# Layer 1's projection for pairs of tiles: seven block products in place of eight

## The chip, the cores and the metric

The kernel runs on one core of one Trainium2 chip. A core has TensorE (PE; its weight loads are shown apart as PEld), VectorE (DVE), ScalarE (ACT), GpSimd (POOL), SyncE (SP) that issues ordinary transfers, and 16 DMA engines which all queues share. SBUF is the working memory, PSUM is where TensorE writes[...]. The metric is the device time of one execution in microseconds; before the change the median of three runs is 1902.05 (1896.26 to 1904.1). The profile is of one further execution that took 1954.92.

## The reference

Two graph-attention layers with a residual and a layer norm each, over N = 3327 nodes with D = 1024 features. `adj` is a 0/1 matrix of some 16 neighbours a node, with a full diagonal.

```python
# layer 0: 8 heads of 128
h = (x @ W).reshape(C, H, D)
e = alpha_src[:, :, None] + alpha_dst[:, None, :]      # then leaky relu, -inf where adj == 0
out = jnp.einsum('hij,hjd->hid', softmax(e), h_heads)
x = _layernorm(x + out)
# layer 1: one head of 1024
h = input @ W
f1 = h @ a1; f2 = h @ a2
attention = softmax(where(adj > 0, leaky_relu(f1 + f2.T), neg), axis=1)
x = _layernorm(x + relu(attention @ h))
```

Since attention @ (x @ W) = (attention @ x) @ W, the kernel aggregates layer 1's inputs first and projects the result.

## The kernel before, in words

Rows are worked on in NT = 26 tiles of P = 128. The program has three stages: a projection for layer 0 that also turns `adj` into lists of neighbours (to about 480 us of the profile), layer 0 (to about 1223), and layer 1 (to the end). A fourth, dense branch isn't taken on this input. All order is written by hand (`tc.manual_schedule()`): each engine gets its instructions in the order in which the program emits them and works on them in that order, waiting on semaphores.

Layers 0 and 1 have one frame, `pipeline` (L1058 on). A tile's neighbours come in four blocks of 4 x 128 rows and one last block of 128 (b = 0 to EB = 4). In the loop of tile t, step b does this, in this order: at b = 0 it closes tile t-1; at b = 2 it prepares tile t+1; it makes the weights of the next block (`weights(b + 1)`, on VectorE, or block 0 of tile t+1 at b = 4); it sums the block (`sums(b)`, on TensorE); it fetches block b of tile t+1 (`fetch`, indirect gathers on POOL, L817, into five buffers); and it runs pieces of the work that is left from tile t-1, written as generators: `run(work, behind[b])` advances it by so many steps. A second queue, `ahead`, is advanced by one step after each block.

In layer 1 (`class Target`, L960):

- `prepare` (L966): a transpose on TensorE of the tile's scores (L969), Exp on ScalarE into `way`, a PSUM bank (L971), the 0/1 marks of the targets on VectorE (`marks`, L833 and L837), and the load of the tile's own row of `y_d` into `res` (L976, SP). `own` has another Exp (L982).
- `weights` (L994): three VectorE operations, two in `way` (L1001, L1002) and one into `es` (L1004).
- `sums` (L1007): 12 matmuls (24 records) for blocks 0 to 3, three (six records) for block 4, into three banks `acc` of tag "A", which has five; the thirds come in the order 2, 0, 1 (L1013).
- `close` (L1018): three small VectorE operations (L1021 to L1023), three ScalarE scalings of `res` into `z` (L1027), three VectorE operations that add the sums (L1030). A third of `acc` is free once its L1030 has read it.
- `finish` (L1035): `z` is transposed in two halves (L176 on TensorE, L179 on ScalarE, one bank of tag "T"), and projected with `wt1`, the 1024 x 1024 weights: for each half of the columns eight matmuls of 128x128 by 128x512 into the one bank of tag "S" (L1045), in pieces of two; then relu and residual in one VectorE operation (L1048) into `o`, a buffer of tag "z".
- `settle` (L1053), queued in `ahead`: the layer norm by `norm_steps` (statistics L192 to L194 and a Sqrt on ScalarE L195 in the first step; reciprocal and normalization, L197 and L199, in the second), then the output DMA on SP.

The call `pipeline(Target, 1, (2, 2, 2, 2, 1), ...)` gives ten pieces a loop: the two transposes after block 0, four matmuls after each of the blocks 1 to 3, two after block 4, and two more after the next tile's `close`.

`score_weights` (L781), queued in `ahead` at the beginning of layer 0, multiplies `wt1` by layer 1's two score vectors, and puts them into `wa`, which layer 0's `finish` uses (L951). Layer 0's tiles use two banks of tag "A" each and one of "S".

Of the kernel before, what the change touches and what calls it, by code (L numbers as in the profile page):

```python
# [9 lines left out]
F32 = mybir.dt.float32  # L10
# [3 lines left out]
AF = mybir.ActivationFunctionType  # L14
OP = mybir.AluOpType
# [4 lines left out]
P = 128  # L20
# [6 lines left out]
def kernel(  # L27
# [28 lines left out]
    nc = tc.nc  # L56
# [100 lines left out]
    class Phase:  # L157
# [10 lines left out]
        def sbuf(self, tag, shape, bufs, name=None, dt=F32):  # L168
            return self.pool.tile(shape, dt, tag=tag, name=name or tag, bufs=bufs)
# [571 lines left out]


    def sparse(own):
        ph = Phase(own, "sparse", {"A": 5, "S": 1, "T": 1, "E": 1})
        pool, bank, sbuf = ph.pool, ph.bank, ph.sbuf
        NS = 5
        srcs = [pool.tile([P, NG, HG], F32, bufs=1, name=f"src{n}") for n in range(NS)]
# [28 lines left out]


        wc = pool.tile([P, 2, KT], F32, bufs=1, name="wc")
        wa = [pool.tile([P, D], F32, bufs=1, name=f"wa{n}") for n in range(2)]

        def score_weights():  # L781
            for n, a in enumerate((a1_src, a1_dst)):
                av = sbuf("z", [P, D], 3, "av")
                spread(av, a)
                for k in range(KT):
                    pr = sbuf("pr", [P, D], 1)
                    nc.vector.scalar_tensor_tensor(
                        pr, wt1[:, k, :], 1.0, av, op0=OP.mult, op1=OP.mult, accum_out=wc[:, n, k : k + 1]
                    )
                    if k % 3 == 2:  # L790
                        yield
                for g in range(2):
                    tr = bank("T", [P, 4, P], "tr")
                    for k in range(4):
                        nc.tensor.transpose(
                            tr[:, k, :], wc[:, n, 4 * g + k : 4 * g + k + 1].to_broadcast([P, P]), ident
                        )
                    nc.scalar.activation(wa[n][:, g * HALF : (g + 1) * HALF], tr.rearrange("p a b -> p (a b)"), AF.Copy)
                yield
# [40 lines left out]
        class Layer0:  # L840
# [5 lines left out]
            def prepare(self):  # L846
                self.re = listed.pop(self.t)
                self.oh, self.oh2 = marks(self.t)
                self.y = ys[self.t % 3]
                load_rows(self.y[:, :D], x, self.t)  # L850
                self.h = sbuf("own", [P, HW0], 2)
                nc.sync.dma_start(self.h, h0_d[self.t * P : (self.t + 1) * P, :])

            def own(self):
# [17 lines left out]
            def weights(self, b):  # L872

                s = self.src[b]
                ng, wide = (NG, GT) if b < EB else (1, P)
                blk = slice(b * NG, b * NG + ng)
                oh = self.oh[:, blk, :] if b < EB else self.oh2.unsqueeze(1)
                wp = way[:, (b % 4) * NG * H : (b % 4 * NG + ng) * H].rearrange("p (g h) -> p g h", g=ng)
                nc.vector.tensor_tensor(wp, s[:, :, D : D + H], self.re[:, blk, :], OP.mult)
                nc.vector.tensor_tensor(wp, wp, s[:, :, D + H : D + 2 * H], OP.max)  # L880
                w = sbuf("w", [P, NG, H], 4)
                nc.scalar.activation(w, wp if b < EB else wp.to_broadcast([P, NG, H]), AF.Copy)  # L882
                e = sbuf("e", [P, H * P], 3).rearrange("p (g h t) -> p g h t", g=ng, h=H)
                nc.vector.tensor_tensor(  # L884
                    e, oh.unsqueeze(2).to_broadcast([P, ng, H, wide]),
                    wp.unsqueeze(3).to_broadcast([P, ng, H, wide]), OP.mult,
                )
                self.made[b] = w, e
# [42 lines left out]
            def finish(self):  # L931

                met = sbuf("met", [NG * H, P], 2)
                nc.vector.tensor_tensor(met, self.den[: NG * H, :P], meets, OP.mult)
                nc.tensor.matmul(self.den[:, P:], met, heads, start=True, stop=True)  # L935
                yield
                ri = sbuf("ri", [P, H], 2)
                nc.vector.tensor_tensor(ri, self.den[:, P:], self.es, OP.add)  # L938
                nc.vector.reciprocal(ri, ri)
                t, row = self.t, self.y  # L940
                y = row[:, :D]
                for h in range(H):
                    yh = y[:, h * DH : (h + 1) * DH]
                    nc.vector.scalar_tensor_tensor(
                        yh, self.acc[h // 4][:, h % 4, :], ri[:, h : h + 1], yh, op0=OP.mult, op1=OP.add
                    )
                yield
                yield from ph.norm_steps([y])
                for n in range(2):
                    pr = sbuf("pr", [P, D], 1)  # L950
                    nc.vector.scalar_tensor_tensor(  # L951
                        pr, y, 1.0, wa[n], op0=OP.mult, op1=OP.mult, accum_out=r1.sd[:, t, n, :]
                    )
                    if n == 0:
                        yield
                nc.scalar.activation(row[:, D + 1 : D + 2], r1.d[:, t, :], AF.Exp)
                nc.scalar.activation(row[:, D + 2 : D + 3], r1.d[:, t, :], AF.Exp, scale=SLOPE)
                nc.sync.dma_start(y_d[t * P : (t + 1) * P, :], row)

        class Target:  # L960
# [4 lines left out]

            def prepare(self):  # L966
                t = self.t
                tr = bank("T", [P, P], "tr")
                nc.tensor.transpose(tr, r1.s[:, t, :].to_broadcast([P, P]), ident)  # L969
                self.r = way[:, (t % 2) * P : (t % 2 + 1) * P].rearrange("p (g t) -> p g t", g=NG)  # L970
                nc.scalar.activation(  # L971
                    self.r.rearrange("p g t -> p (g t)"), tr, AF.Exp, scale=1 - SLOPE
                )
                self.oh, self.oh2 = marks(t)
                self.res = ys[t % 3]
                nc.sync.dma_start(self.res, y_d[t * P : (t + 1) * P, :])  # L976

            def own(self):
# [10 lines left out]
                self.src[b] = gather(y_d, HW, self.t, b)  # L989

            def begin(self):
                self.acc = [bank("A", [P, CUTS[1]], "acc1") for _ in range(3)]

            def weights(self, b):  # L994
                s = self.src[b]
# [22 lines left out]
            def close(self):  # L1018
# [2 lines left out]
                nc.vector.tensor_tensor(ri[:, 2:3], self.acc[2][:, D - CUTS[2] : D - CUTS[2] + 1], self.es[:, :1], OP.add)  # L1021
                nc.vector.reciprocal(ri[:, :1], ri[:, 2:3])
                nc.vector.tensor_tensor(ri[:, 1:2], ri[:, :1], self.es[:, :1], OP.mult)  # L1023
                z = self.z = sbuf("z", [P, D], 3)
                for c in (2, 0, 1):
                    cut = slice(CUTS[c], min(CUTS[c + 1], D))
                    nc.scalar.activation(z[:, cut], self.res[:, cut], AF.Copy, scale=ri[:, 1:2])  # L1027
# [6 lines left out]

            def finish(self):  # L1035

                t, z, res = self.t, self.z, self.res
                xT = sbuf("xT", [P, KT, P], 2)
                yield from ph.transposed(xT, z, (0, 1))
                o = sbuf("z", [P, D], 3, "o")  # L1040
                for g in range(2):
                    half = slice(g * HALF, (g + 1) * HALF)
                    acc = bank("S", [P, HALF], "mm")
                    for k in range(KT):
                        nc.tensor.matmul(acc, xT[:, k, :], wt1[:, k, half], start=k == 0, stop=k == KT - 1)  # L1045
                        if k in (1, 3, 5):
                            yield
                    nc.vector.scalar_tensor_tensor(o[:, half], acc, 0.0, res[:, half], op0=OP.max, op1=OP.add)  # L1048
                    if g == 1:
                        ahead.append(self.settle(o))  # L1050
                    yield

            def settle(self, o):  # L1053
                yield from ph.norm_steps([o])
                for r in pieces(self.t):
                    nc.sync.dma_start(out[at(self.t, r), :], o[r])

        def pipeline(kind, late, behind, get):  # L1058

            tiles = [kind(t) for t in range(NT)]
            work = deque()
            get(0)
            tiles[0].prepare()
            for b in range(EB + 1):
# [2 lines left out]
            for t, tg in enumerate(tiles):  # L1070
                tg.begin()
                for b in range(EB + 1):
                    if b == 0 and t:
                        tiles[t - 1].close()
                        run(work, late)
                    if b == 0 and t + 1 < NT:
                        get(t + 1)
                    if b == 2 and t + 1 < NT:
# [7 lines left out]
                    tg.sums(b)  # L1086
                    if t + 1 < NT:
                        tiles[t + 1].fetch(b)
                    run(work, behind[b])
                    if t or b:  # L1090
                        run(ahead)
                if t == 0 and late:
                    work.append(iter(range(1)))
                work.append(tg.finish())
            tiles[-1].close()
            run(work, late)
            run(ahead, -1)
            run(work, -1)
            run(ahead, -1)

        with tc.manual_schedule():
            pipeline(Layer0, 0, (1, 1, 1, 1, 1), get_edges)
            pipeline(Target, 1, (2, 2, 2, 2, 1), lambda t: None)


    def by_pairs(own):
# [145 lines left out]
```

## Time and profile before

| what | value |
|---|---|
| median of three runs | 1902.05 us |
| the profiled execution | 1954.92 us, its span 1953.2 us |
| busy, whole span | PE 1668.2 us (85%), DVE 1151.9 (59%), ACT 546.6 (28%), POOL 1039.7 (53%) |
| granted TensorE clock, mean | 0.907 |
| projection matmuls of layer 1 (L1045) | 832 records, 382.3 us busy, 603 ns each, overlapping |
| sums of layer 1 (L1013), blocks 0 to 3 | 2496 records, 215.9 us busy |
| gathers of layer 1 (L817) | 416 and 26, 1002 and 990 ns of POOL each |
| data read from and written to HBM | 578.85 and 42.97 MB |

A record is one hardware instruction; an fp32 matmul has two. Times of matmuls overlap each other, so what a group of them costs is read from its start to the next group's. The chain of waits is followed back from the last instruction: each entry was released by the one before it, so an engine that fills the chain sets the time. "Idle before" in a group's row counts only where nothing else was late. "Granted clock" is the share of the full TensorE clock in a stretch.

### The profile page before, as it was taken

To read this page: it belongs to the slowest core of one execution; us is meant where nothing else is said; L and a number is where in the kernel's file an instruction comes from. 1 tells how busy PE (TensorE), PEld (TensorE's weight loads), DVE (VectorE), ACT (ScalarE), POOL (GpSimd) and SP (SyncE) were. 2 spreads that over 40 slices of the span, in tenths; PEclk is the share of its full clock that TensorE was granted. 3 is DMA by queue.
4 is the path that set the end of the run, shared out by engine and by line. 5 is a ranking of instruction groups with operands and counts; after the bars stand their busy time and mean duration, and the time that the engine had idled before them with its cause. 6 is when DMAs were issued, how large, how long until landed. Compare 5 with 4: busy or idle time off the path is not lost.

```text
span 1953.2 us, 36865 instructions
## 1 busy us (share of the span) xinstructions
PE 1668.2 (85%) x14091; PEld 915.1 (47%) x14091; DVE 1151.9 (59%) x3087; ACT 546.6 (28%) x1422; POOL 1039.7 (53%) x1391
## 2 busy tenths in 40 slices
PE   8799999997577787777877777479999999999997
PEld 5456555564444554544454445134444444444343
DVE  6699989985575566556665566134444444444442
ACT  5445554442122222222222222012122222222221
POOL 4322222211666666666666663566666666666650
PEclk9899999998677887879787887589999999999999
DMA  7556554311999999999999996899999999999980
GB/s 183 95 129 130 112 94 92 88 60 64 404 356 377 370 365 387 381 372 363 379 377 375 369 371 225 335 318 386 378 378 367 381 366 373 357 377 368 355 340 32
DMA packets 171063, 567.68 MB, mean 291 GB/s; under 512 B 27690, under 2 KB 34346, under 8 KB 170878
## 3 DMA queue, kind: packets, MB, share of 16 engines
q0 software_dynamic: 131056, 455.68, 67.3%
q1 hardware_dynamic: 39822, 109.56, 15.1%
q8 instruction: 113, 1.85, 0.4%
q14 instruction: 72, 0.59, 0.1%
HBM read 578.85 MB, written 42.97 MB: 318 GB/s over the span
## 4 chain that ended last, share of the span: by engine, by line
PE 74%; issue 10%; DVE 6%; ACT 5%; DMA 2%; another core or an unknown queue 1%; POOL 1%; SPq 0%; POOLq 0%; DVEq 0%; ACTq 0%
PE mm L1045 19%; PE acc L914 19%; PE acc L1013 13%; PE mm L479 12%; PE acc L906 4%; PE acc L896 3%; ACT junk L311 3%; PE tr L176 2%; DMA wt<-in_L_gnn_W_dram 1%; DMA src<-h_d,idx 1%; PE den L922 1%; PE xp L411 1%; DVE top L274 1%; PE den L935 1%
## 5 line engine op out<-in xcount | busy, mean ns | idle before, releaser
L817 POOL DMA_INDIRECT src<-h_d,idx x416 | 448.9, 1079 | 228.0 <-PE acc L914 83.1
L817 POOL DMA_INDIRECT src<-y_d,idx x416 | 416.8, 1002 | 250.9 <-issue 84.4
L914 PE MATMUL acc<-src,e 128*32 128x128 f32 x6656 | 396.2, 321 | 167.0 <-issue 138.1
L914 PEld LDWEIGHTS acc<-src,e 128*32 128x32 f32 x6656 | 254.1, 127 | 332.5 <-issue 309.4
L479 PE MATMUL mm<-wt,xT 128*128 128x347 f32 (+1 forms) x1248 | 402.0, 468 | 3.0 <-DMA wt<-in_L_gnn_W_dram 2.6
L1045 PE MATMUL mm<-wt,xT 128*128 128x512 f32 x832 | 382.3, 603 | 3.1 <-DVE o L1048 3.1
L479 PEld LDWEIGHTS mm<-wt,xT 128*128 128x128 f32 x1248 | 228.2, 192 | 105.5 <-issue 4.0
L1013 PE MATMUL acc<-src,es 128*32 128x342 f32 (+1 forms) x2496 | 215.9, 467 | 39.2 <-DVE es L1004 24.9
L1045 PEld LDWEIGHTS mm<-wt,xT 128*128 128x128 f32 x832 | 151.9, 190 | 201.6 <-issue 184.9
L884 DVE TENSOR_TENSOR e<-oh,way 128x1024 f32<-128x1024 f32 x130 | 158.7, 1221 | 110.0 <-ACT w L882 29.5
L1013 PEld LDWEIGHTS acc<-src,es 128*32 128x32 f32 x2496 | 73.6, 112 | 171.5 <-issue 163.4
L882 ACT ACTIVATE w<-way 128x32 f32<-128x32 f32 x130 | 25.0, 193 | 449.1 <-PE acc L914 177.2
L1027 ACT ACTIVATE z<-y,ri 128x342 f32<-128x342 f32 (+1 forms) x78 | 39.5, 569 | 290.5 <-issue 118.7
L1001 DVE TENSOR_TENSOR way<-way,src 128x128 f32<-128x128 f32 x104 | 31.1, 299 | 147.2 <-ACT way L971 57.1
L1048 DVE SCALAR_TENSOR_TENSOR o<-mm,y 128x512 f32<-128x512 f32 x52 | 35.9, 691 | 108.9 <-PE mm L1045 73.9
L179 ACT ACTIVATE xT<-tr 128x512 f32<-128x512 f32 x104 | 59.4, 596 | 128.0 <-PE tr L176 115.0
L906 PE MATMUL acc<-own,ident 128*128 128x512 f32 x104 | 81.0, 871 | 0.0
L311 ACT ACTIVATE junk<-ad 128x3328 uint8<-128x3328 uint8 x26 | 78.4, 3014 | 2.5 <-POOL ad L308 2.5
L1021 DVE TENSOR_TENSOR ri<-acc,es 128x1 f32<-128x1 f32 x26 | 4.1, 158 | 124.3 <-PE acc L1013 116.7
L938 DVE TENSOR_TENSOR ri<-den,es 128x8 f32<-128x8 f32 x26 | 4.3, 166 | 119.8 <-PE den L935 119.8
L296 POOL CAST mvs<-r 128x8 bf16<-128x8 f32 x26 | 6.1, 235 | 122.8 <-ACT r L295 122.8
L864 ACT ACTIVATE own<-own,es 128x128 f32<-128x128 f32 x208 | 63.6, 388 | 26.2 <-DVE es L861 16.0
(194 smaller groups left out, 2020.8 us busy)
## 6 DMA issues: line engine op xcount, KB each, us to landing
h_d<-ht SPq DMA_DIRECT2D x26, 520.0 KB
own<-h_d SPq DMA_DIRECT2D x26, 520.0 KB
y_d<-y SPq DMA_DIRECT2D x26, 514.0 KB
y<-y_d SPq DMA_DIRECT2D x26, 514.0 KB
x<-in_x_dram SPq DMA_DIRECT2D x25, 512.0 KB
y<-in_x_dram SPq DMA_DIRECT2D x25, 512.0 KB
out_dram<-o SPq DMA_DIRECT2D x25, 512.0 KB
ad<-in_adj_dram POOLq DMA_DIRECT2D x25, 415.9 KB
```

The lines of the kernel that those rows point to most:

```text
L179: nc.scalar.activation(part, tr, AF.Copy)
L311: nc.scalar.activation(junk, ad, AF.Copy, accum_out=self.deg)
L479: nc.tensor.matmul(acc, xT[t][:, k, :], wt[:, k, CUTS0[c] : CUTS0[c + 1]], start=k == 0, stop=k == KT - 1)
L817: nc.gpsimd.indirect_dma_start(out=s[:, g, :w], out_offset=None, in_=table[:, :], in_offset=bass.IndirectOffsetOnAxis(ap=idx[:, t, b * NG ...
L864: nc.scalar.activation(hn, hn, AF.Copy, scale=es[:, n : n + 1])
L884: nc.vector.tensor_tensor(e, oh.unsqueeze(2).to_broadcast([P, ng, H, wide]), wp.unsqueeze(3).to_broadcast([P, ng, H, wide]), OP.mult,)
L896: nc.tensor.matmul(self.acc[h // 4][:, h % 4, :], e[:, 0, h, :], rowsof[:, 0, h, :], start=False, stop=h % 4 == 3,)
L906: nc.tensor.matmul(self.acc[b - 1].rearrange("p h d -> p (h d)"), ident, self.h[:, (b - 1) * HALF : b * HALF], start=False, stop=False,)
L914: nc.tensor.matmul(self.acc[h // 4][g * GT : (g + 1) * GT, h % 4, :], e[:, g, h, :], rowsof[:, g, h, :], start=first and h % 4 == 0, stop= ...
L1013: nc.tensor.matmul(self.acc[c][to, :m], es[:, g, :], s[:, g, CUTS[c] : CUTS[c + 1]], start=b == 0, stop=b == EB,)
L1027: nc.scalar.activation(z[:, cut], self.res[:, cut], AF.Copy, scale=ri[:, 1:2])
L1045: nc.tensor.matmul(acc, xT[:, k, :], wt1[:, k, half], start=k == 0, stop=k == KT - 1)
```

## The change

For two tiles a (even) and b (odd), the rows of a and b, cut into two halves of the 1024 inputs, are a 2 x 2 matrix of blocks, and so are the weights (w11, w12, w21, w22, each 512 x 512). The plain product needs eight products of blocks, each four matmuls; the change uses a Strassen form with seven (28 matmuls for a pair instead of 32), with sums and differences of blocks before and after them:

- `combine_weights`, once between the layers on VectorE: t3 = w22 - w12, w12 becomes w12 - w11, t2 = w22 - w12 (new), t4 = w21 - t2; w12 is overwritten in place. The other results lie in buffers that layer 0 has done with (`e`, `prod`, `own`), which therefore become named tiles.
- The even tile does two products, a1 w11 and a2 w21, and can put its first half at once. The odd tile does five, with s1 = b1 + b2, s2 = s1 - a1, b1 = a1 - b1, and s2 = a2 - s2 as new left operands, and puts its own halves and the even tile's second.
- `put` replaces L1048 by two VectorE operations: the sum of two partial results (one in PSUM) and the relu with the residual, in place in `res`. So `o` goes; `z` has one buffer; the residual rows have five (the three `ys` and the two `wa` of layer 0).
- Tag "A" has four banks in place of five, "S" two in place of one. `acc` takes its banks in the order 2, 0, 1. The transpose of `prepare` writes a part of `way`.
- `pipeline` takes a plan: for even and odd t, and for six places (after `close`, and after each block), which left-over tile is advanced: "even" and "odd" are the last tile of each kind that is complete. An even tile's six pieces run over loops t+1 and t+2, an odd tile's twelve over t+1 and t+2. After the last tile, two more rounds of the plan are run.

```diff
-        ph = Phase(own, "sparse", {"A": 5, "S": 1, "T": 1, "E": 1})
+        ph = Phase(own, "sparse", {"A": 4, "S": 2, "T": 1, "E": 1})
...
+        def combine_weights():
+            for n in range(2):
+                k = slice(2 * n, 2 * n + 2)
+                nc.vector.tensor_tensor(t3[n], w22[:, k, :], w12[:, k, :], OP.subtract)
+            nc.vector.tensor_tensor(w12, w12, w11, OP.subtract)
+            for n in range(2):
+                k = slice(2 * n, 2 * n + 2)
+                nc.vector.tensor_tensor(t2[n], w22[:, k, :], w12[:, k, :], OP.subtract)
+                nc.vector.tensor_tensor(t4[n], w21[:, k, :], t2[n], OP.subtract)
...
             def prepare(self):
                 t = self.t
-                tr = bank("T", [P, P], "tr")
+                tr = way[:, 3 * P :]
...
-                self.res = ys[t % 3]
+                self.res = y1s[t % len(y1s)]
...
-                self.acc = [bank("A", [P, CUTS[1]], "acc1") for _ in range(3)]
+                self.acc = {c: bank("A", [P, CUTS[1]], "acc1") for c in (2, 0, 1)}
...
             def finish(self):
...
-                acc = bank("S", [P, HALF], "mm")
-                for k in range(KT):
-                        nc.tensor.matmul(acc, xT[:, k, :], wt1[:, k, half], start=k == 0, stop=k == KT - 1)
-                    nc.vector.scalar_tensor_tensor(o[:, half], acc, 0.0, res[:, half], op0=OP.max, op1=OP.add)
...
+                self.xT = sbuf("xT", [P, KT, P], 2)
+                turn = ph.transposed(self.xT, self.z, (0, 1))
+                next(turn)
+                yield
+                next(turn)
+                yield from self.second() if self.t % 2 else self.first()
+
+            def product(self, a, w):
+                self.p = bank("S", [P, HALF], "mm")
+                for k in range(HK):
+                    nc.tensor.matmul(self.p, a[:, k, :], w(k), start=k == 0, stop=k == HK - 1)
+                    if k == 1:
+                        yield
+
+            def put(self, g, u, p, room):
+                half = slice(g * HALF, (g + 1) * HALF)
+                nc.vector.tensor_tensor(room, u, p, OP.add)
+                nc.vector.scalar_tensor_tensor(
+                    self.res[:, half], room, 0.0, self.res[:, half], op0=OP.max, op1=OP.add
+                )
+
+            def first(self):
+                yield
+                yield from self.product(self.xT, lambda k: w11[:, k, :])
+                nc.scalar.activation(u2, self.p, AF.Copy)
+                yield
+                yield from self.product(self.xT[:, HK:, :], lambda k: w21[:, k, :])
+                self.put(0, u2, self.p, u4)
+                yield
+
+            def second(self):
+                before = tiles1[self.t - 1]
+                a, b = before.xT, self.xT
+                a1, a2, b1, b2 = a[:, :HK, :], a[:, HK:, :], b[:, :HK, :], b[:, HK:, :]
+                nc.vector.tensor_tensor(s1, b1, b2, OP.add)
+                nc.vector.tensor_tensor(s2, s1, a1, OP.subtract)
+                nc.vector.tensor_tensor(b1, a1, b1, OP.subtract)
+                yield
+                yield from self.product(s2, lambda k: t2[k // 2][:, k % 2, :])
+                nc.vector.tensor_tensor(u2, u2, self.p, OP.add)
+                nc.vector.tensor_tensor(s2, a2, s2, OP.subtract)
+                yield
+                yield from self.product(s1, lambda k: w12[:, k, :])
+                p5 = self.p
+                nc.vector.tensor_tensor(u4, u2, p5, OP.add)
+                yield
+                yield from self.product(b1, lambda k: t3[k // 2][:, k % 2, :])
+                nc.vector.tensor_tensor(u3, u2, self.p, OP.add)
+                self.put(1, u3, p5, u2)
+                yield
+                yield from self.product(b2, lambda k: t4[k // 2][:, k % 2, :])
+                self.put(0, u3, self.p, u3)
+                ahead.append(self.settle())
+                yield
+                yield from self.product(s2, lambda k: w22[:, k, :])
+                before.put(1, u4, self.p, u4)
+                ahead.append(before.settle())
+                yield
...
-        def pipeline(kind, late, behind, get):
+        def pipeline(tiles, plan, get):
+            left = []
+
+            def rest(t, n):
+                for who in plan[t % 2][n]:
+                    k = {"before": t - 1, "even": t - 2 + t % 2, "odd": t - 1 - t % 2}[who]
+                    if 0 <= k < len(left):
+                        next(left[k], None)
...
                         tiles[t - 1].close()
-                        run(work, late)
+                        rest(t, 0)
...
-                    run(work, behind[b])
+                    rest(t, b + 1)
...
+            for t in (NT, NT + 1):
+                for n in range(EB + 2):
+                    rest(t, n)
+                    run(ahead)
             run(ahead, -1)
...
-            pipeline(Layer0, 0, (1, 1, 1, 1, 1), get_edges)
-            pipeline(Target, 1, (2, 2, 2, 2, 1), lambda t: None)
+            one = ("before",)
+            pipeline([Layer0(t) for t in range(NT)], (((),) + (one,) * 5,) * 2, get_edges)
+            combine_weights()
+            tiles1 = [Target(t) for t in range(NT)]
+            y1s = ys + was
+            e, o = "even", "odd"
+            pipeline(
+                tiles1, (((e,), (o, e), (o, e), (o, o), (o, o), ()), ((o, o), (e, o), (e, o), (o,), (o, e), ())),
+                lambda t: None,
+            )
```

## The prediction

> **What bounds the kernel now.** I began with the page's busy tenths. Layer 1 is the last third of the span.
>
> ```profile
> PE   8799999997577787777877777479999999999997
> PEclk9899999998677887879787887589999999999999
> DMA  7556554311999999999999996899999999999980
> ```
>
> In layer 1 TensorE and the DMA engines are both at nine tenths, at full clock, so two resources compete to be the bound. The chain of waits over one tile tells which one it is (start us, length, what):
>
> ```profile
> 1587.68 3.43 PE mm L1045 x8
> 1591.11 1.86 PE acc L1013 x24
> 1592.97 0.59 PE tr L176 x4
> 1593.56 0.69 issue
> 1594.25 0.66 PE tr L176 x4
> ...
> 1600.40 0.11 PE tr L969
> ...
> 1611.49 1.73 PE acc L1013 x6
> 1613.22 0.86 PE mm L1045 x2
> ```
>
> The chain never leaves TensorE: a tile is 25.54 us (1587.68 to 1613.22), with one stall of 0.69 us between the two transposes. An fp32 matmul shows as two records, so 3.43 us is four matmuls: 0.857 us each. A group of four that directly follows the sums takes 3.63. How near DMA is, and how the clock reacts to idleness, come from stretches of the trace (length; busy us of PE, PEld, DVE, ACT, POOL; granted clock, DMA share, GB/s):
>
> ```profile
> 1331.19:1586.63 255.44, 247.81 (x1428) 106.04 (x1427) 114.02 (x330) 58.37 (x100) 170.07 (x170) 1.00 0.99 374
> ...
> 1248.90:1252.30 3.40, 1.44 (x10) 0.49 (x7) 1.69 (x5) 0.00 (x0) 2.48 (x4) 1.00 1.02 406
> 1252.30:1255.70 3.40, 1.81 (x3) 0.28 (x3) 0.00 (x0) 0.00 (x0) 2.79 (x3) 0.50 1.02 406
> ...
> 1839.30:1842.70 3.40, 1.79 (x4) 0.87 (x5) 2.36 (x7) 0.00 (x0) 1.94 (x2) 1.00 1.04 420
> ```
>
> Ten tiles move 374 x 255.44 = 95.5 MB, 9.55 MB a tile. At the 408 GB/s that backlogged stretches reach, the DMA floor is 23.4 us a tile: TensorE is the bound by only 2.1 us. PE busy for 1.44 of 3.40 us was followed by a stretch at half clock; the stretch with 1.79 of 3.40 still had the full clock, and so had what followed.
>
> **What decides on VectorE.** The third view is the timeline around one tile's preparation:
>
> ```profile
> 1622.69 1.28 ACT L971 ACT_TABLE_LOAD   x1
> ...
> 1629.50 0.26 ACT L971 ACTIVATE way<-tr 128x128 f32<-128x128 f32 x1 [5.53 <-PE acc L1013]
> 1629.80 0.30 DVE L1001 TENSOR_TENSOR way<-way,src 128x128 f32<-128x128 f32 x1 [5.36 <-issue]
> ```
>
> In nearly every tile the weights of block 3 (L1001 to L1004, 0.95 us) start 0.03 us after ScalarE's Exp for the next tile (L971), which itself needs a table load after a Sqrt. Today nothing is lost: sums(3) stands behind four matmuls. The page's row for the operation that the change multiplies:
>
> ```profile
> L1048 DVE SCALAR_TENSOR_TENSOR o<-mm,y 128x512 f32<-128x512 f32 x52 | 35.9, 691 | 108.9 <-PE mm L1045 73.9
> ```
>
> [...] 691 here, 1221 for the 1024-wide L884. [...]
>
> **The change, part by part**, for a pair of tiles (before: 2 x 25.54 = 51.08 us).
>
> TensorE: 28 matmuls for 32: -4 x 0.857 = -3.43. The two transposes of a tile come in different blocks, so the 0.69 us stall goes: -1.38. Groups directly behind sums fall from six to four (-0.4), and six two-matmul groups appear, which may cost as much: 0.
>
> VectorE: 15 operations of 512 replace 4: 10.4 us for 2.8, +7.6 a pair. Busy goes from 45% to some 60%: not a bound, but it is in order, and three places matter.
>
> 1. Odd loop, after product 4 (in block 1). VectorE: start 0.1, add 0.72, relu-add 0.72, then at once the settling's statistics (1.7), done at 3.24. ScalarE: Sqrt to 3.5, Exp table 1.28, Exp 0.26, to 5.1. Then weights(3) 0.95: sums(3) can start at 6.15. TensorE meanwhile has L969 0.11, sums(2) 1.86, and just one half product, 1.91: 3.88. Stall 2.27. Were the Exp not waited for, VectorE's own order (statistics, marks 1.0, weights) still gives 5.2: stall 1.3.
> 2. Odd to even. After product 5: put 1.54, statistics 1.7, weights(0) 0.95, reciprocal and norm 1.0: `close` starts at 5.2 and frees its first bank at 6.95 (three small operations 0.58, z 0.61 and 0.57 later). TensorE arrives at the second third of sums(0), which with four banks needs that bank, at 1.75 + 1.73 + 1.71 + 0.62 = 5.81. Stall 1.2.
> 3. Even loop, block 0: u2's copy (0.6) and a table load precede the Exp of `own`, so weights(1) is late by 0.3.
>
> Other blocks have slack: in the even loop sums(3) could start at 6.8 and is reached at 8.1; product 4's bank is free at 5.1 for 6.0. Stalls are 3.77, so a pair takes 51.08 - 4.81 + 3.77 = 50.04: -1.04, over 12 pairs **-12.5**.
>
> Clock: a gap of 2.27 us takes over 1.8 us out of one window (below the 0.52 busy that was tolerated) in (1.14 + 0.94)/3.41 = 61% of positions: 7 of 12 gaps. A half-speed window loses 1.7: **+11.9** (0 if such gaps are tolerated, +41 if each of the 12 costs two windows).
>
> Start: loop 1 had groups of 4.28, 3.63 and 3.63 (chain, from 1288.56); one half group of 1.9 and a moved transpose (about 1) stay. Its gathers were all issued by 1275.5, so the gain is real: **-8.5** (0 if DMA still holds the loop). The work isn't saved, it moves to the end.
>
> End: before, from the last tile's sums (1922.78) to the end of the last normalization (1948.70) 25.9. After, in order: half product 1.86, wait for the late z 2.6, transposes 1.24, two half products 3.42, wait for s2 0.4, three products 10.3, wait for the bank that p5 holds 1.6, two products 6.86, then VectorE: remains of one settling 1.1, put 1.54, statistics 1.7, Sqrt 0.3, norm 1.0. Together 33.9: **+8.0** (+6 to +11).
>
> At nothing: combining the weights (6 x 1.22 + 2.29 = 9.6 us of VectorE) falls where VectorE waits 15.17 us for the first gather (1238.88); uncovered, +9.6. Layer 0 with four banks uses two a tile, freed two blocks into the next; two S banks and its new plan issue the same steps: 0, at most 1 us a tile. SP issues the same DMAs; both outputs of a pair now leave within one odd loop, behind that loop's load of y: 1 MB, 2.6 us of DMA, covered by the four blocks of gathers in flight. POOL is 17 x 1.29 = 21.9 us a tile, unchanged.
>
> Sum: -12.5 + 11.9 - 8.5 + 8.0 = -1.1 on the profiled 1954.92 (span 1953.2), which stands 2.8% above the median 1902.05. Scaled: **1901**.
>
> **Rivals.** (B) *The stalls are covered.* For it: VectorE is 45% busy and I priced each operation at its full length, while the trace shows starts 0.61 apart. Against: the chain at 1 is fixed by dependencies. A pair would take 46.27, 23.1 a tile; DMA's 23.4 takes over, realistically 23.5: -2.04 x 24 = -49, 1854; with half the stalls 1878.
> (C) *Slower, by the clock.* Every gap at place 1 pulls the clock down for two windows: 12 x 3.4 = +41, less 12.5: 1929. For it: layer 0, with PE 77% busy, was granted 0.81. Against: TensorE is busy right after each gap. Each window costs 1.7 us, so the loops' gain is gone at 7 windows, and from 13, more than one a pair, it is slower.
> (D) *DMA sets the pace* and the removed matmuls change nothing: loops 0, start 0, end +8, 1910. For it: the share of 0.99. Against: the chain holds no gather, and POOL waits for PE to free buffers.
>
> **Chances.** A measurement of this kernel tells about 0.5%, 9.5 us: faster below 1892.5, slower above 1911.5. A, the forecast, 0.45 (own range 1888 to 1914: 0.09 faster, 0.27 same, 0.09 slower). B 0.24, faster. C 0.26 (0.24 slower). D 0.05 (0.04 same). Faster 0.33, same 0.33, slower 0.34. Range 1864 to 1926: it leaves out the lower half of B and the top of C.
>
> **What would show it.** Right: in odd loops L1013 waits about 2 us for L1004 once a pair; in even loops about 1 us for the z operations of `close` (L1030); the clock at 0.5 now and then in layer 1; a pair near 51 us with the drops; DMA share below 0.99. Wrong: a steady clock of 1.00 and a pair at 47 (B), DMA named as the releaser ahead of L1004 (D), or waits of TensorE for a product's bank in every loop, which I price at 0.

## The result, and the profile after

The kernel after the change takes 1897.69 us (median of 12 runs, 1892.61 to 1902.04), the kernel before 1900.43 (12 runs, 1896.26 to 1904.1): a ratio of 0.9988 [0.9977, 0.9999]. The forecast was 1901. The 2.7 us between them are less than the 0.5% below which the prediction calls two times the same.

Chips differ here, and it matters for what follows. The first group of experiments below comes from a chip on which the kernel before takes 1948 us; all other runs, those of after included, come from chips on which it takes 1900. For the profile of before that the prediction worked from (1954.92 us) no chip is on record; its layer 0 takes 746.9 us, near the 740.6 of that first chip and not the 712 to 723 of all others, so it most likely comes from there. The kernel before was not profiled on a chip where it takes 1900, so what is said of its loops and its end is measured on the slower one. Every experiment's ratio compares runs on one chip.

The profiled execution of after took 1897.84 us, its span 1896.1. Its page, in busy tenths of 40 slices (the last 15 slices are layer 1):

```profile
PE   8799999999356666766766656389999999999997
PEclk9899999999688878878787888599999999999999
DMA  7666455411899999999999997899999999999971
```

TensorE and DMA still share the nines. The chain of waits over the part of an odd loop that the prediction calls place 1 (start us, length, what):

```profile
1290.16 1.73 PE mm L1083 x4
1291.91 0.70 DVE u L1090
...
1293.37 1.30 DVE st L192 x2
...
1295.34 1.28 ACT L1006
1296.63 0.27 ACT way L1006
...
1297.60 0.30 DVE es L1039
1297.94 1.93 PE acc L1048 x24
```

Before, the chain never left TensorE in a tile. Now it leaves it twice a pair. The first time it goes by the predicted way and in the predicted order: put, statistics, the Exp table's load, Exp, weights(3), sums(3). The second time follows some ten us later, over the normalization to the late `close`, as predicted too:

```profile
1306.00 0.81 DVE y L199
...
1308.64 1.36 PE acc L1048 x16
```

The waits between 1250 and 1850 us (who waits in which line for what: us in total, times, longest) show both stalls:

```profile
PE acc L1048 <- DVE es L1039: 25.5, 12, 2.3
PE acc L1048 <- DVE z L1065: 10.8, 12, 1.0
```

There are twelve waits for weights(3), eleven of 2.17 to 2.29 us and the first one of 1.45, and twelve for the z operations of `close`, 0.94 us as a rule. No wait of TensorE for a bank of a product is among the larger ones. The clock in this trace is 1.00 or 0.50 and changes 123 times in the whole program, always on one grid whose step is 3.413 us (3.4133, within 0.004 us); in the loops of layer 1 each drop lasts one step. What a gap did to the clock is read from stretches of 3.41 us, laid on those edges (length; busy us of PE, PEld, DVE, ACT, POOL; granted clock, DMA share, GB/s):

```profile
1548.79:1552.20 3.41, 1.33 (x20) 0.68 (x24) 2.23 (x8) 2.30 (x3) 2.66 (x3) 1.00 1.02 396
1552.20:1555.61 3.41, 3.41 (x15) 1.18 (x4) 0.37 (x2) 0.00 (x0) 2.50 (x4) 0.50 1.01 405
...
1599.98:1603.39 3.41, 1.67 (x24) 0.68 (x24) 2.51 (x8) 1.97 (x3) 2.80 (x3) 1.00 0.97 315
1603.39:1606.80 3.41, 3.41 (x12) 1.55 (x9) 1.22 (x3) 0.00 (x0) 2.50 (x4) 1.00 0.97 351
```

The gap that left 1.33 us of work in its stretch was followed by a stretch at 0.50; the one that lies across an edge, and left 1.67, was not. Nine of the eleven gaps of full length were followed by such a drop; in the three further profiles of this kernel (below) eight of eleven. The same columns for nine pairs of tiles, for one without a drop and for one with:

```profile
1345.02:1801.34 456.32, 428.00 (x2502) 179.06 (x2502) 267.77 (x694) 109.36 (x190) 311.11 (x310) 0.97 0.99 380
1599.55:1648.79 49.24, 46.09 (x278) 19.48 (x278) 29.74 (x78) 12.15 (x22) 35.34 (x35) 1.00 1.00 379
1548.69:1599.55 50.86, 47.74 (x279) 19.98 (x278) 29.72 (x78) 12.16 (x22) 33.22 (x33) 0.97 0.98 376
```

A pair takes 456.32 / 9 = 50.70 us, against 51.08 before (on the slower chip): 49.24 without a drop, 50.86 with one, so that a drop cost 1.62.

### The profile page after: what moved, and what is told of

Its sections match the earlier page's. It is cut to its first block, busy times and chain, and to the rows that moved or that the text cites. A ratio compares the mean times of both kernels' runs of the same rounds, so it can differ in the third digit from the quotient of the medians.

```text
span 1896.1 us, 36779 instructions
## 1 busy us (share of the span) xinstructions
PE 1521.5 (80%) x13987; PEld 878.8 (46%) x13987; DVE 1253.0 (66%) x3237; ACT 550.2 (29%) x1433; POOL 1034.4 (55%) x1391
## 3 DMA queue, kind: packets, MB, share of 16 engines
q8 instruction: 112, 1.84, 0.4%
## 4 chain that ended last, share of the span: by engine, by line
PE 45%; DMA 23%; DVE 17%; ACT 8%; issue 5%; POOL 2%; DVEq 0%; SPq 0%; POOLq 0%; ACTq 0%
DMA src<-h_d,idx 17%; PE mm L479 13%; PE mm L1083 13%; PE acc L1048 9%; PE acc L950 5%; DMA src<-y_d,idx 3%; DVE e L920 3%; ACT junk L311 3%; PE tr L176 2%; DVE st L192 2%; POOL src L853 2%; DMA wt<-in_L_gnn_W_dram 1%; DVE y L199 1%; PE xp L411 1%; PE acc L942 1%
## 5 line engine op out<-in xcount | busy, mean ns | idle before, releaser
L853 POOL DMA_INDIRECT src<-h_d,idx x416 | 440.8, 1060 | 209.6 <-PE acc L950 63.9
L950 PE MATMUL acc<-src,e 128*32 128x128 f32 x6656 | 268.8, 329 | 120.0 <-DVE e L920 120.0
L950 PEld LDWEIGHTS acc<-src,e 128*32 128x32 f32 x6656 | 228.3, 134 | 194.9 <-DVE e L920 114.8
L479 PEld LDWEIGHTS mm<-wt,xT 128*128 128x128 f32 x1248 | 227.9, 192 | 105.3 <-issue 3.8
L1048 PE MATMUL acc<-src,es 128*32 128x342 f32 (+1 forms) x2496 | 219.8, 484 | 70.4 <-DVE es L1039 58.6
L1048 PEld LDWEIGHTS acc<-src,es 128*32 128x32 f32 x2496 | 73.1, 114 | 217.9 <-issue 115.9
L915 DVE TENSOR_TENSOR way<-src,re 128x32 f32<-128x32 f32 x104 | 21.1, 202 | 139.7 <-DMA src<-h_d,idx 101.7
L971 PE MATMUL den<-heads,met 32*128 32x8 f32 x52 | 13.4, 328 | 114.7 <-DVE met L970 114.7
L1083 PE MATMUL mm<-wt,s 128*128 128x512 f32 x208 | 104.9, 639 | 0.0
L1083 PE MATMUL mm<-wt,xT 128*128 128x512 f32 x208 | 97.9, 593 | 0.0
L1090 DVE TENSOR_TENSOR u<-u,mm 128x512 f32<-128x512 f32 x52 | 35.6, 685 | 89.5 <-PE mm L1083 89.0
L195 ACT ACTIVATE sg<-sg 128x1 f32<-128x1 f32 x52 | 10.6, 203 | 200.4 <-DVE sg L194 200.4
```

The source lines that it names most:

```text
L479: nc.tensor.matmul(acc, xT[t][:, k, :], wt[:, k, CUTS0[c] : CUTS0[c + 1]], start=k == 0, stop=k == KT - 1)
L853: nc.gpsimd.indirect_dma_start(out=s[:, g, :w], out_offset=None, in_=table[:, :], in_offset=bass.IndirectOffsetOnAxis(ap=idx[:, t, b * NG ...
L950: nc.tensor.matmul(self.acc[h // 4][g * GT : (g + 1) * GT, h % 4, :], e[:, g, h, :], rowsof[:, g, h, :], start=first and h % 4 == 0, stop= ...
L1048: nc.tensor.matmul(self.acc[c][to, :m], es[:, g, :], s[:, g, CUTS[c] : CUTS[c + 1]], start=b == 0, stop=b == EB,)
L1083: nc.tensor.matmul(self.p, a[:, k, :], w(k), start=k == 0, stop=k == HK - 1)
```

## The experiments

The theory after the result: seven products do save TensorE time, and two places on VectorE (place 1 and the late `close`) give most of it back, directly (2.17 + 0.94 us a pair) and by the clock (1.6 us for a drop). Rivals: DMA holds the pace and TensorE's gaps are idle time that would be lost anyway; or the stalls cost only their own length and the clock nothing.

**1. Take the late work away from the two places, and the kernel before once more** (the chip where before takes 1947.92 us).

`ahead` holds the settlings. These three kernels skip its step at one block of the odd loops, so that statistics or norm come a block later (each has one of the last three lines):

```diff
-        def pipeline(tiles, plan, get):
+        def pipeline(tiles, plan, get, hold=()):
...
-                    if t or b:
+                    if (t or b) and (t % 2, b) not in hold:
                         run(ahead)
...
+                hold=((1, 1),),               # settle later
+                hold=((1, 4),),               # norm later
+                hold=((1, 1), (1, 4)),        # both later
```

The kernel before, unchanged:

> The kernel before, profiled once more, because its first profile (1954.92 us) stands 2.8% above its median. All theories: about 1900 us; in layer 1 a tile of 25.54 us as in the first profile, at a clock of 1.00; the 50 us that are missing were lost ahead of layer 1's loops. It shows layer 1's start (first gather to the loop of tile 2), which I priced at 8.5 us more than after the change, and its end (25.9 us from the last sums to the last normalization).

It took 1945.82 us, and its tiles again 25.54 us with 0.69 between the transposes.

The settling's statistics out of place 1:

> The changed kernel, with the odd tile's settling begun one block later, so that its statistics and Sqrt come after the Exp of the next tile's preparation and after the weights of block 3. Stall theory: the stall of 2.17 us ahead of sums(3) goes, and with it every drop of the clock in layer 1 (1.6 us each, 10 or so): a pair falls from 50.8 to about 47.2 us, 12 pairs, some 40 us: 1857 (1850 to 1870). The stall of 0.94 stays. DMA theory (the gathers can't be faster): TensorE waits for gathers instead, the pair stays above 49.5, 1885 or more. VectorE theory (15 operations of 0.69 us a pair are too many, wherever they stand): the wait moves to another block, 1890.

The norm out of place 2:

> The changed kernel, with the last step of the even tile's settling (reciprocal and normalization, 1.0 us) held until after the next tile's close. Stall theory: close starts 1.0 us earlier, the stall of 0.94 us in even loops goes, the one of 2.17 with its clock drops stays: 12 x 0.9 = 11 us less if the clock drops as often, 1887 (1878 to 1892; the drops depend on where the gap meets the clock's window, so 4 fewer or 4 more are possible, 6 us each way). DMA or VectorE theory: no change, 1897.

Both:

> Both of these changes. Stall theory: no stall of TensorE above 0.5 us is left in the loops, clock 1.00, TensorE alone would need 46.3 us a pair; the DMA floor is 23.4 us a tile, so a pair is 46.8 to 47.2 and gathers begin to be late now and then: 1850 (1842 to 1862). DMA theory: no better than 1885.

All three missed, and by much: 1972.21 us, ratio 1.0126 [1.0097, 1.0154]; 1968.21, ratio 1.0102 [1.0081, 1.0124]; and 1953.39, ratio 1.0021 [1.0005, 1.0038]. Their traces have something that the one after, on its chips, does not show, and the kernel before hardly. In the timeline of the last one (start us, length, engine, line, operation; idle before and its releaser):

```profile
1747.81 0.66 PE L176 MATMUL tr<-ident,z 128*128 128x128 f32 x4
...
1751.59 0.60 ACT L179 ACTIVATE xT<-tr 128x512 f32<-128x512 f32 x1 [8.00 <-PE acc L1048]
```

The copy of the transpose starts 3.1 us after the transpose's recorded end (1748.47), where in the runs on the other chips it mostly starts 0.04 us after. Over the 52 copies of layer 1 this delay is 1.32, 0.98 and 1.24 us in the mean of the three kernels, and half of the copies are more than 0.3 us late; in the repeated run of before on the same chip four are, and the mean is 0.16. Pairs of tiles vary from 49 to 57 us in the three kernels, while those of any kernel on the other chips lie within 3 us of each other. A matmul's end is modelled in the records, so TensorE may really have run later than they say; what slowed it on this chip was not found, and the kernel after itself was not run on it.

There is also a flaw in the edit. `run(ahead)` goes on to the next generator in the queue when one is used up, so after the first hold, the norm of one settling and the statistics of the next ran in one step, ahead of `close`. The first hold thus moves part of a stall instead of removing it.

**2. The change, idle time filled, the old transposes, both holds in single steps** (before: 1900.13 us). All four on one chip. First the kernel after, for comparison:

> The changed kernel as it is, beside the kernel before on one chip, since the two profiles came from executions that differ by some 50 us in layer 0 too (a gather packet 176 ns long on average there against 171). Theory 1 (a chip's gathers decide how much of the change is kept): on a chip where the kernel before takes about 1948 the changed kernel is 15 to 25 us slower than it, and in layer 1 the operations that wait for TensorE start 1 to 3 us after its recorded end, as in the three variants just run; on one where it takes 1900 the ratio is 0.999. Theory 2 (the variants themselves made it worse): 0.999 on either.

It took 1897.87 us, ratio 0.9988 [0.9977, 0.9998].

Then TensorE does useless work where it has to wait: the first matmul of the product with w22, which lies ahead of the gap at place 1, is done three times, 26 matmuls more in all.

```diff
-            def product(self, a, w):
+            def product(self, a, w, again=0):
                 self.p = bank("S", [P, HALF], "mm")
+                for _ in range(again):
+                    nc.tensor.matmul(self.p, a[:, 0, :], w(0), start=True, stop=True)
...
-                yield from self.product(s2, lambda k: w22[:, k, :])
+                yield from self.product(s2, lambda k: w22[:, k, :], again=2)
```

> The changed kernel with two matmuls more in the odd tile's last product: its first matmul is done three times, the first two results being overwritten, so that TensorE works for 1.7 us of the gap ahead of sums(3). If the drops of the clock cost 1.6 us each and the gap is fixed by VectorE's chain: the gap shrinks to 0.5 us, no drop is left in the loops, a pair goes from 50.8 to 49.2 us, 12 us less than the changed kernel although it does 26 matmuls more. If the chain is not the limit: 26 x 0.86 = 22 us more.

It took 1883.76 us, ratio 0.9923 [0.9902, 0.9944]: with more work it is 14.1 us faster than the kernel after on the same chip. The eight drops in the profile of the kernel after there are worth 13 at 1.6 us each. Its stretch of nine pairs and its waits for the weights:

```profile
1343.08:1786.50 443.42, 430.31 (x2539) 182.18 (x2538) 268.00 (x694) 109.40 (x190) 312.83 (x310) 1.00 1.01 391
```

```profile
PE acc L1048 <- DVE es L1039: 4.2, 9, 0.6
```

The clock stays at 1.00, the wait shrinks from 2.17 to about 0.46 us, and a pair takes 443.42 / 9 = 49.27: what the kernel after has in a pair without a drop (49.24). The price of the gap beyond its own length is the clock's. The rival that the clock costs nothing is out.

The other saving of the change, the transposes in different blocks, alone in the kernel before:

```diff
-            pipeline(Target, 1, (2, 2, 2, 2, 1), lambda t: None)
+            pipeline(Target, 1, (1, 3, 2, 2, 1), lambda t: None)
```

> The kernel before with the plain eight products, but with its two transposes in two blocks (one after block 0, the other with four matmuls after block 1), which the change also does. The stall of 0.69 us a tile goes: 25 x 0.69 = 17 us less, 0.991 of before, if TensorE is the bound; if the gathers are (24.85 us a tile against a floor of 23.4), less than half of it.

1874.78 us, ratio 0.9872 [0.9854, 0.9891]: 25 us faster than the kernel before, and 23 faster than the change. Its tiles take 24.59 us with no gap:

```profile
1350.00:1800.00 450.00, 450.00 (x2637) 194.66 (x2636) 210.00 (x610) 107.59 (x184) 312.50 (x314) 1.00 1.01 391
```

I had expected 25 x 0.69 = 17 us. Against 25.54 (on the slower chip) the tile is shorter by 0.95. The chains of the two kernels show where the 0.26 beyond the stall come from: the four matmuls of block 1 now follow a transpose and not the sums, and take 3.44 us in place of 3.63, and the second transpose takes 0.59 in place of 0.66. DMA did not hold it back: the eight products move 391 GB/s as soon as TensorE asks for them.

Last, both holds as in the first group, but with one step of `ahead` at each block and no more:

```diff
+            def one_step():
+                if ahead:
+                    try:
+                        next(ahead[0])
+                    except StopIteration:
+                        ahead.popleft()
...
-                    if t or b:
-                        run(ahead)
+                    if (t or b) and (t % 2, b) not in hold:
+                        if hold:
+                            one_step()
+                        else:
+                            run(ahead)
...
+                hold=((1, 1), (1, 4)),
```

> The changed kernel with the settlings of the odd loop held back as in the run with both changes, but a step of the second settling can no longer follow in the same place as the last step of the first (in that run both stood ahead of close, so its stall of 0.98 remained). Stall theory: neither stall is left, clock 1.00, a pair of 46.8 to 47.5 us, 35 to 45 us less than the changed kernel beside it. Gather theory: TensorE's work a pair is then 46.3 us against 46.8 for the gathers at their best, so waits for gathers replace the stalls, and no more than a third of that gain is seen.

1862.03 us, ratio 0.98 [0.978, 0.9819]: the best of all kernels here, 36 us under the kernel after on the same chip. Ten pairs, and what is waited for in them:

```profile
1343.33:1817.54 474.21, 461.21 (x2779) 195.44 (x2779) 293.82 (x768) 121.66 (x208) 342.36 (x334) 1.00 1.01 398
```

```profile
DVE way L1036 <- DMA src<-y_d,idx: 68.2, 26, 4.6
```

47.42 us a pair, no drop of the clock, and now the weights wait for gathers, which the kernel after did four times in a longer stretch (9.8 us). The chain of waits over this stretch spends 36.9% of its time in gathers. The rival that DMA holds the pace becomes true here, in part, and only here. The stretch moves 398 GB/s, where the kernel after moves 380 over its nine pairs.

**3. One place alone, on chips where before takes 1900 us.** The same edits as in the first group. Place 1 (before: 1900.82):

> The variant with the odd tile's settling begun one block later once more, now that chips are known to differ: on the first, operations started 1 to 3 us after TensorE's recorded end in the three variants, and not in the kernel before. On a chip where the kernel before takes 1900: the stall ahead of sums(3) and the clock drops are gone; but statistics and norm of both settlings now stand ahead of close, so the other stall grows from 0.94 to 1.9: a pair 50.8 - 1.6 - 2.2 + 1.0 = 48.0 us, about 34 us below the changed kernel, 1864. On one where it takes 1948: 1.01 of before, as measured.

1872.18 us, ratio 0.9851 [0.9824, 0.9879]. The kernel after beside it:

> The changed kernel beside it on the same chip. Where before takes 1900: 0.999 of before. Where it takes 1948: if the chip's gathers decide, the late starts after TensorE's recorded ends are there too, and it is 15 to 25 us slower than before (1.01); if the late starts belong to the variants, it is 0.999 of before and starts are on time.

1897.7, ratio 0.9985 [0.9973, 0.9997]. So the hold gains 25.5 us on the kernel after and 28.6 on the one before, where on the first chip it lost 24 against the one before. Its waits from 1350 to 1800 us:

```profile
PE acc L1048 <- DVE z L1065: 18.6, 10, 1.9
```

The stall at place 1 is gone, and the one for `close` has doubled from 0.94 to 1.86 us, the flaw named above; one gap of 1.86 a pair brings no drop here (the clock is 1.00 from 1350 to 1800 us). A pair takes 47.89 us.

Place 2 (before: 1900.26), and the kernel after a third time:

> The variant that holds back the even tile's normalization until after close, once more. Where before takes 1900: the stall of 0.94 us a pair goes, the gap of 2.17 with its clock drops stays: 11 us below the changed kernel if the clock drops as often (8 times in 12), 1887; the drops can be from 4 fewer to 4 more, 6 us each way. Where before takes 1948: 1.01 of before, as measured.

> The changed kernel beside it. Where before takes 1900: 0.999. Where it takes 1948: 1.01 if the chip's gathers decide, with starts 1 to 3 us after TensorE's recorded ends; 0.999 with starts on time if those belonged to the variants.

1875.17, ratio 0.9868 [0.9852, 0.9885], beside 1897.99, ratio 0.9991 [0.9982, 1.0]. I had expected 11 us from it, 12 x 0.94, and it gained 23. The gaps at place 1 are as they were:

```profile
PE acc L1048 <- DVE es L1039: 19.7, 9, 2.3
```

```profile
1350.00:1800.00 450.00, 429.80 (x2574) 181.31 (x2573) 276.28 (x718) 113.58 (x197) 322.81 (x317) 0.99 1.01 395
```

But of eleven such gaps only three, two of them in this window, halve the clock (0.99 in the mean, not 0.97), against eight in the kernel after on the same chip. Five drops fewer at 1.6 us are another 8 us. Some 3.5 us remain; in the two profiles layer 0, which the edit leaves alone, differs by 4.5 us (714.5 and 719.0).

**Why the gaps hit so often.** The grid of 3.413 us on which the clock of after changes is one and the same through the whole program, in layer 0 as in layer 1: the half-speed stretches begin at 1347.4, 1398.6, 1449.8, 1501.0 and 1552.2, 51.2 = 15 x 3.413 apart. A pair of after with a drop takes about 50.86. With a drop, the gap therefore meets almost the same place in a step every time. Its start, less the beginning of the nearest step, is 1.03, 0.67, 0.49, 0.26 and -0.10 us for the five gaps from 1345.02 on, all with a drop; then -0.43 (1599.55), without one. The pair that follows is short (49.24), which puts the next gap at 1.03 again, and the cycle begins anew: five of six. The three further profiles of the kernel after have the same cycle in the length of sums(3) behind the gap, on the first: 1.93 us (full clock), then 3.62, 3.34, 3.10, 2.74 and 2.40, as the half-speed stretch begins later and later in it. With place 2 mended a pair without a drop takes 48.33 us, 0.54 more than 14 steps, so the gap starts 0.54 us later in its step each time until it is hit (starts of 0.02, 0.00 and 0.34 us were). The pair with the drop takes 49.92, 1.28 less than 15 steps, and it is two or three pairs before the gap is back: three hits in eleven. This working fits the profiles; no run sets the length of the loop alone. How idle a step has to be was not shown: here 1.33 us of work in 3.41 (0.39) was followed by a drop, and 1.67 (0.49) was not, but the recorded work alone does not tell them apart, since a stretch with 1.43 us (1636.03 to 1639.44) was not followed by a drop in the run with place 2 mended, while the one with 1.44 in the prediction was.

## Why the prediction was right

| term of the sum | predicted | measured |
|---|---|---|
| stall at place 1, a pair | 2.27 us | 2.17 |
| stall for `close`, a pair | 1.2 | 0.94 |
| third stall (even loop, block 0) | 0.3 | no gap of TensorE |
| pair without a drop | 50.04 | 49.24 |
| one drop of the clock | 1.7 | 1.62 |
| gaps with a drop | 7 of 12 | 9 of 11 (8 of 11 in three further profiles) |
| mean pair | 51.03 (50.04 + 11.9 / 12) | 50.70 over nine pairs, 8 of them with a drop |
| end, last sums to last normalization | 33.9 | 32.35 |

**The stalls** are the predicted ones, at the predicted places. The two that exist are smaller by 0.36 us together and the third doesn't show; that is 0.66 of the 0.80 by which the pair is shorter.

**The clock** was right in kind and size, too low in number. Step "61% of positions" was an estimate that takes the gaps to fall anywhere in a stretch of 3.41 us (the trace of before has such a grid too: all 85 changes of its clock lie whole steps of 3.413 us apart); in after five of six gaps kept to -0.10 to 1.03 us from the beginning of a step, and were hit. Nine drops at 1.62 are 14.6 us in place of 11.9, while the shorter pair is worth -0.8 x 12 = -9.6. The loops gain 12 x 1.84 - 14.6 = 7.5 us where the sum had 0.6.

**The end** is longer by 32.35 - 27.45 = 4.9 us than in the repeated run of before, where +8.0 was predicted: my "after" was near, and "before" was 25.75 us in the profile that I used. The chip makes no difference here: the eight products with split transposes take 27.44 on a faster one.

**The start** gains on the slower chip only. From the first gather of layer 1 to the end of loop 1's sums, before takes 77.0 us in the profile of the prediction and 76.2 in the repeated run; the three variants of the change on that chip take 69.8 to 70.9, so some 6 of the 8.5 us are there. On the faster chips the four profiles of the kernel after take 57.5 to 58.6, and the eight products with split transposes 58.5: nothing is left to gain. The -8.5 was read from a slow start that these chips do not have. That fits the sum: after the loops (-7.5) and the end (+4.9), about nothing is left of the measured -2.7. It takes the 51.08 us a pair from the slower chip.

**Luck.** The terms are off by -9.6 (the pair), +2.7 (the drops), -3.1 (the end) and some +8.4 (the start). That the forecast lies within 3.3 us of the measured time is owed to these cancelling each other; the stalls, their places, the clock and the end are what it had right. One of its signs did not show: the DMA share is 0.99 over the nine pairs, not below it.

**At nothing.** Combining the weights takes from 1193.04 to 1202.6 us on VectorE (six operations of 1.22 to 1.26 us and one, 2048 wide, of 2.29), and the first weights of layer 1 start at 1210.71, after a wait of 7.2 us for the first gather: hidden, as predicted. Layer 0 takes 715.74 us in the kernel after and 712.1 in the one with split transposes on the same chip; three more profiles of the kernel after have 717 to 719, so a cost of a few us is possible and not shown. Output and load of y in one loop: no wait names them.

**The scale.** Scaling from 1954.92 to the median treated the 2.8% as an evenly spread cost of that execution. It most likely is the chip, and sits in layer 0 and the start: layer 0 takes 740.56 us in the repeated run of before, 712 to 723 with all kernels on the other chips. Since the predicted difference was only -1.1 us, nothing came of it.

**The rivals.** B (stalls covered, 1854 with DMA as the bound, 1878 with half of the stalls): not what the change does, since the chain at place 1 is bound by dependencies, as said. It is what the holds in single steps make of it: 1862.03, with 23.7 us a tile where B had 23.5, and gathers waited for. There the product saved is worth something: 12.8 us under the eight products with split transposes, on the same chip. C (slower by the clock): its mechanism is at work, with one stretch of 3.41 us a gap, not two. D: out in the kernel after, whose stretches with a drop move 376 GB/s where the holds in single steps draw 398.

## What to carry to other kernels

A saving on the bounding engine is worth its length less the stalls that the new work brings on others, and less what those stalls do to the clock. Here a gap of 2.17 us a pair, in pairs of 50.86 us beside 51.2 for 15 of the clock's steps, was followed by half the clock nine times of eleven: look for such a gap before changing the arithmetic. Postponing steps of the settling, for which no engine was waiting, was worth 36 us here; the change itself, with one product in eight less, 2.7. And take the comparison on the same chip: one edit gained 1.5% on one and lost 1.3% on another.

## What the hardware showed that I had not expected

- 26 more matmuls, put where TensorE had to wait, made the program 14.1 us faster, by keeping the clock at 1.00.
- Pairs of 50.86 us kept almost in step with the 3.413 us on which the clock of after changes (15 make 51.2): five of six gaps were followed by half the clock; with pairs of 48.33 us, three of eleven were.
- Chips differ by 2.5% for the same kernel (1947.92 and 1900.13 us), and not evenly: layer 0, in which the DMA engines are busy for 0.97 of the time, took 740.56 us against 712.1 with the same code, while a tile of layer 1 takes 25.54 us on the slower chip, and on a faster one 24.59 with the transposes split, a difference that the chains account for without the chip.
- On the slower chip, three kernels had copies of transposes that start 1.0 to 1.3 us in the mean, and up to 6 us, after the recorded end of the transpose they wait for; in the kernel before the mean was 0.16. The cause is open, and so is whether the kernel after suffers from it there.
